# A graph layer on one core: a slot's rows loaded and split chunks ahead, and two small products placed behind slot products in TensorE's order

## The chip, the core and the metric

The kernel runs on one core of one Trainium2 chip. A core has five engines that run beside each other and wait for one another by semaphores: TensorE (PE) multiplies matrices, VectorE (DVE) and ScalarE (ACT) work element by element, GpSimd (POOL) here mostly issues indirect DMAs that gather rows, and SyncE (SP) issues plain DMAs. Each engine runs its own instructions strictly in the order in which they stand in its queue; an instruction that waits holds up all behind it. The metric is the device time of one execution in microseconds (us), the median of several runs.

## The reference

```python
def _L0_gnn_ref(x, src, dst, theta_w, theta_b, phi_w, phi_b):
    x_src = x[src]
    x_dst = x[dst]
    theta_x = (x_dst - x_src) @ theta_w.T + theta_b
    phi_x = x_src @ phi_w.T + phi_b
    e = jax.nn.relu(theta_x + phi_x)
    out = jax.ops.segment_max(e, dst, num_segments=x.shape[0])
    return jnp.where(jnp.isfinite(out), out, 0.0)
x = _layernorm(x + _L0_gnn_ref(x, src, dst, ...), axis=-1)
```

There are 6250 nodes of 256 float32 features and 100000 edges, sorted by destination. Every node takes the maximum, over its incoming edges, of a linear function of both ends, adds it to itself, and is normalised.

## The kernel before

**The algebra.** What an edge adds that depends on its source is one row, B[source] = x[source] @ (phi - theta).T. The part that depends on the destination is the same for all edges of a node and is added after the maximum. So the kernel makes B once (the DRAM tensor `b_rows`), and then needs, per node, the maximum of B over its sources.

**Three ways to the maximum.** The first 618 nodes ("part 1") gather one row per edge: `gather_group` issues indirect DMAs on POOL, eight steps to a group, and `run_steps` (L696) runs a capped maximum along the steps on DVE, 81 steps in all. The other 5632 nodes are served by **slots** and by the **list**. A slot is a block of 383 rows of B; there are 17. For each slot and each of these nodes at most one edge is chosen, and its row is fetched by a product with a one-hot matrix; the maximum is kept in `acc`. Edges that no slot took go to the list, which is gathered like part 1, 257 steps.

**A slot.** `slot_terms(s)` (L1063) loads the slot's rows from `b_rows` into `raw` (SP, L1078; one buffer), splits them into a rounded part (ACT, L1082) and the rest (DVE, L1083), and keeps both in `terms` (two buffers). `slot_halves(s, c)` then works on one **chunk** of the nodes: chunks 0 to 4 have 1024 nodes and chunk 5 has 512. It loads the chosen row numbers (`want`, three buffers), makes the one-hot tile `hot` (two buffers; ACT L1102 and L1105, or DVE L1100 for one block out of three once `dve_hots` is set), and for each half h of the features multiplies `terms` by `hot` into a PSUM tile `ps_f` (three buffers; 12 matmuls for a half of a wide chunk, 6 for a half of chunk 5; L1113), which DVE merges into `acc` (L1124; ACT L1122 in slot 0). I write "slot 2, chunk 0, half 1" for such a piece; slots count from 0. Of each block's two terms the rounded part is multiplied first, so the first two matmuls of a half need only ACT's part, and the third needs DVE's.

**The list's front.** While slots 0 to 3 run, DVE also finishes part 1's steps and builds the list (`list_pieces`): a sum over lists (`sums_of_lists`, two small matmuls at L1151 and L1152, whose result `list_chunks` reads), a compaction of a table of 1584 entries (L1244, L1254), a DMA of the compacted words (L1263), three indirect DMAs that fetch each partition's run of words (`dst_w`, L519), and DVE's merge of these (L1275 to L1286), whose result `list_src` releases the list's 256 gathers on POOL.

**The end of part 1.** `tails_1` takes the last row of each partition through TensorE (L905), a scan on DVE (L907) and a cap (L910), back through TensorE (L914) and into `carried` (ACT, L916), which `heads_1` uses at L925, after the list has begun.

**What sets the order.** The calls are written in one program order, but the framework that builds the program arranges each engine's queue itself, by its own estimate of when each operand is there. `behind_in_order(one, name, reason)` adds an order without a wait: `one` stands behind `name` on its engine. In the list's phase (`pinned`) the list's steps and the slots' merges on DVE are tied to each other in that way, and `halves_until` spreads the slots' pieces over the list's steps. At the end POOL gathers the 44 tiles' results from `maxima_2` and DVE and ACT normalise them.

## Time and profile before

| | before |
|---|---|
| runs | 739.37, 734.26, 736.09 us, median 736.09 |
| profiled execution | 738.83 us, of which the span of the core's instructions 737.0 us |
| PE / DVE / ACT / POOL busy | 90% / 86% / 72% / 72% of the span |
| mean granted clock of TensorE | 0.955 |
| slot matmuls (L1113) | 2156, 519.9 us busy |
| DMA | 167.06 MB, 227 GB/s over the span |

The page of the profile gives busy shares, the costliest groups of instructions with the idle time ahead of them, and the chain of work that ended last. A timeline row has start and length in us, the engine, the line of the kernel, the operation with its output and input tiles, the number of instructions merged into it, and in brackets the idle time ahead of it and what ended it. Since instructions overlap in an engine's pipeline, a row's length can be more than the distance to the next row's start. A row of a table by stretches has the stretch, its length, the busy time of PE, of its weight loads, of DVE, ACT and POOL with instruction counts, then the granted clock, the share of DMA and its GB/s.

### The profile page before, as it was taken

How to read it: one execution, taken by the hardware profiler on the slowest of the kernel's cores; microseconds unless marked ns; L12 is line 12 of the kernel's file. 1: busy time of each engine (PE TensorE's matmuls, PEld its weight loads, DVE VectorE, ACT ScalarE, POOL GpSimd, SP SyncE). 2: the span in 40 equal slices, each digit the busy share in tenths (PEclk: the TensorE clock that was granted, in tenths of full speed). 3: DMA queues.
4: the chain of work that ended last, by engine and by line, in shares of the span. 5: the costliest groups of instructions: out<-in, count | busy, mean ns of one | idle time of the engine just before them, and what ended most of it. 6: DMA issues, size and time to landing. Idle time of an engine off the chain costs nothing.

```text
span 737.0 us, 9895 instructions
## 1 busy us (share of the span) xinstructions
PE 661.5 (90%) x2908; PEld 536.1 (73%) x2908; DVE 630.5 (86%) x1193; ACT 532.7 (72%) x611; POOL 529.1 (72%) x730
## 2 busy tenths in 40 slices
PE   5989978679697999999999999999999988979990
PEld 3878756567475888888888888888888876758880
DVE  7999998999996678988989888888888984697885
ACT  1445788788697676967869687876877878852685
POOL 6810477888315848888888888888888888438880
PEclk9999998889798999999999999999999998989995
DMA  8997553737456547777787968786867675555874
GB/s 260 313 360 289 191 165 108 261 101 229 156 194 207 179 143 223 247 217 260 222 277 217 354 218 272 249 312 223 263 211 252 210 243 177 164 187 172 269 279 192
DMA packets 60879, 167.06 MB, mean 227 GB/s; under 512 B 11896, under 2 KB 21905, under 8 KB 54673
## 3 DMA queue, kind: packets, MB, share of 16 engines
q1 hardware_dynamic: 39717, 107.15, 41.6%
q0 software_dynamic: 18976, 52.35, 24.1%
q10 hardware_dynamic: 2124, 6.84, 2.5%
q8 instruction: 25, 0.41, 0.2%
q14 instruction: 37, 0.30, 0.1%
HBM read 102.94 MB, written 63.36 MB: 226 GB/s over the span
## 4 chain that ended last, share of the span: by engine, by line
PE 63%; DVE 11%; DMA 7%; ACT 7%; POOL 6%; issue 6%; SPq 0%; DVEq 0%; POOLq 0%; ACTq 0%
PE ps_f L1113 56%; PE ps_b L791 4%; POOL g L526 4%; DMA x_columns<-x_t 3%; DVE g L696 2%; ACT hot L1102 2%; ACT hot L1105 2%; DMA g<-maxima,place 2%; POOL pause L496 1%; DVE wide L1032 1%; DMA dst_w<-list_words,run_start 1%; DVE words L1244 1%; DVE acc L1124 1%; DMA w_in<-in_L_gnn_theta_w_dram 1%; ACT x_t L779 1%
## 5 line engine op out<-in xcount | busy, mean ns | idle before, releaser
L1113 PE MATMUL ps_f<-hot,terms 128*128 128x512 f32 x2156 | 519.9, 402 | 28.0 <-ACT hot L1105 22.0
L1113 PEld LDWEIGHTS ps_f<-hot,terms 128*128 128x128 f32 x2156 | 412.7, 194 | 128.8 <-ACT hot L1105 31.6
L526 POOL DMA_INDIRECT g<-b_rows,list_src x256 | 258.2, 1009 | 61.0 <-issue 37.3
L1102 ACT ACTIVATE hot<-want,minus_row 128x1024 fp32r<-128x1024 f16 (+1 forms) x224 | 229.0, 1071 | 97.7 <-PE ps_f L1113 97.7
L1124 DVE TENSOR_TENSOR acc<-acc,ps_f 128x1024 f32<-128x1024 f32 x192 | 215.8, 1129 | 69.4 <-PE ps_f L1113 68.6
L1105 ACT ACTIVATE hot<-hot 128x2048 fp32r<-128x2048 f32 (+2 forms) x102 | 196.4, 1925 | 2.5
L696 DVE SCALAR_TENSOR_TENSOR g<-g,caps 128x256 f32<-128x256 f32 x335 | 161.1, 481 | 2.1
L526 POOL DMA_INDIRECT g<-b_rows,src x65 | 89.4, 1376 | 62.8 <-DMA b_rows<-b_sb 43.0
L496 POOL IOTA pause<- 128x160 f32 x312 | 96.9, 311 | 2.3
L791 PE MATMUL ps_b<-weights,x_t 128*128 128x256 f32 x260 | 60.9, 388 | 2.8 <-ACT x_t L779 2.4
L526 POOL DMA_INDIRECT g<-maxima,place x44 | 42.7, 971 | 27.1 <-DMA maxima<-g 20.2
L791 PEld LDWEIGHTS ps_b<-weights,x_t 128*128 128x128 f32 x260 | 48.9, 194 | 11.3 <-ACT x_t L779 5.2
L1100 DVE TENSOR_SCALAR hot<-want,row_id 128x1024 fp32r<-128x1024 f16 (+1 forms) x70 | 52.1, 745 | 0.3 <-issue 0.3
L1363 PE MATMUL ps_e<-weights,kept 128*128 128x256 f32 x176 | 41.6, 379 | 0.0
L1393 ACT ACTIVATE squares<-x_f,r 128x256 bf16<-128x256 f32 x49 | 24.2, 494 | 20.6 <-DVE r L1390 20.6
L1363 PEld LDWEIGHTS ps_e<-weights,kept 128*128 128x128 f32 x176 | 33.4, 190 | 4.3
L794 ACT COPY b_sb<-ps_b 128x512 f32<-128x512 f32 (+1 forms) x25 | 14.4, 578 | 23.4 <-PE ps_b L791 16.8
L779 ACT COPY x_t<-ps_xt 128x512 f32<-128x512 f32 (+1 forms) x33 | 18.5, 588 | 13.1 <-PE ps_xt L776 7.8
L526 POOL DMA_INDIRECT g<-in_x_dram,src x16 | 23.1, 1444 | 5.4 <-issue 4.1
L1408 ACT ACTIVATE x_f<-x_f,r 128x256 f32<-128x256 f32 x41 | 21.4, 588 | 6.8 <-DVE r L1400 3.9
L1373 DVE TENSOR_TENSOR g<-g,ps_e 128x512 f32<-128x512 f32 x22 | 15.1, 686 | 8.7 <-DMA g<-maxima,place 3.5
L519 POOL DMA_INDIRECT dst_w<-list_words,run_start x3 | 3.1, 1048 | 25.8 <-DMA list_words<-work 25.5
(255 smaller groups left out, 429.6 us busy)
## 6 DMA issues: line engine op xcount, KB each, us to landing
maxima<-g SPq DMA_DIRECT2D x42, 1024.0 KB
want<-chosen_rows SPq DMA_DIRECT2D x85, 256.0 KB
x_q<-in_x_dram SPq DMA_DIRECT2D x12, 512.0 KB
b_rows<-b_sb ACTq DMA_DIRECT2D x12, 512.0 KB
x_columns<-x_t SPq DMA_DIRECT2D x22, 256.0 KB
kept<-x_columns SPq DMA_DIRECT2D x11, 512.0 KB
raw<-b_rows SPq DMA_DIRECT2D x16, 256.0 KB
g<-b_rows,list_src POOLq DMA_INDIRECT x256, 4.3
```

Source lines behind the costliest of these rows:

```text
L496: return nc.gpsimd.iota(t, pattern=[[step, t.shape[1]]], base=base, channel_multiplier=per_partition, allow_small_or_imprecise_dtypes=True,)
L526: one = nc.gpsimd.indirect_dma_start(out=to, out_offset=None, in_=table, in_offset=bass.IndirectOffsetOnAxis(ap=offsets, axis=0))
L696: one = nc.vector.scalar_tensor_tensor(g[:, k, :], last[part], caps[:, t : t + 1], g[:, k, :], op0=ALU.min, op1=ALU.max)
L779: nc.scalar.copy(x_t[:, :w], ps[:, :w])
L791: nc.tensor.matmul(ps[:, h, :], x_t[:, h, k, :], weights[:, k, 0, :], start=(k == 0), stop=(k == KC - 1))
L1100: nc.vector.tensor_scalar(hot[:, b, :], want, row_id[:, b : b + 1], None, op0=ALU.is_equal)
L1102: nc.scalar.activation(hot[:, b, :], want, AF.Abs, bias=minus_row[:, b : b + 1], scale=1.0)
L1105: nc.scalar.activation(apart, apart.bitcast(FP), AF.Relu, bias=1.0, scale=-1.0)
L1113: nc.tensor.matmul(ps[:, w : w + 512], terms[:, part, b, h * P : (h + 1) * P], hot[:, b, w : w + 512], start=(i == 0), stop=(i == n - 1),)
L1124: one = nc.vector.tensor_tensor(to, to, ps, op=ALU.max)
L1363: nc.tensor.matmul(a[:, i, :], x_t[:, 2 * i + c, :], weights[:, c, 1, :], start=False, stop=(i == w - 1 and c == KC - 1))
L1393: nc.scalar.activation(squares, x_f[:, k, :], AF.Square, bias=mean[:, k : k + 1], scale=1.0, accum_out=var[:, k : k + 1])
```

## The change

Two things are altered. First, `slot_terms` becomes a generator of two steps, rows and terms: the rows of slot s+1 are asked for at chunk 2 of slot s, its terms at chunk 4 of slot s; before, both were asked for at chunk 0 of the slot itself. Slot 0 still does both at once. Second, two small products on TensorE are issued later in the program and tied behind the latest slot product that has been written: the sums over the lists, and the transposes of the carried rows, which move from `tails_1` to the first step of `heads_1`, inside the list's loop. No instruction is added or removed.

```diff
+ROWS_AT = 2
+TERMS_AT = 4
...
+    latest_product = [None]
...
         nc.vector.memset(capped[:, :, 0:1], -BIG2)
+        return capped
+
+    def heads_1(capped):
         carry = misc()
         for k in range(KC):
-            nc.tensor.transpose(carry[:, k * P : (k + 1) * P], capped[:, k, :], ident)
+            one = nc.tensor.transpose(carry[:, k * P : (k + 1) * P], capped[:, k, :], ident)
+            behind_in_order(one, latest_product[0], "slots ahead of the heads")
         carried = work.tile([P, D], FP, name="carried", bufs=1)
         nc.scalar.copy(carried, carry[:, :D])
-        return carried
-
-    def heads_1(carried):
         heads = work.tile([P, D], FP, name="heads", bufs=1)
...
             if s == 0:
                 behind_in_order(one, x_loaded, "x ahead of a slot's rows")
+        yield
         terms = terms_of[s] = slots.tile([P, PARTS, KB, D], FR, name="terms")
         nc.scalar.copy(terms[:, 0, :n], raw[:, :n])
...
+        yield
+
+    terms_ahead = [None]
 
     def slot_halves(s, c):
-        if c == 0:
-            slot_terms(s)
+        if c == 0 and s == 0:
+            for _ in slot_terms(s):
+                pass
+        if c == ROWS_AT and s + 1 < NS:
+            terms_ahead[0] = slot_terms(s + 1)
+            next(terms_ahead[0])
+        if c == TERMS_AT and s + 1 < NS:
+            next(terms_ahead[0])
         terms, blocks = terms_of[s], blocks_in(s)
...
-                    nc.tensor.matmul(
+                    one = nc.tensor.matmul(
...
+            latest_product[0] = one.ins.name
             to = acc[:, h, begin : begin + wide_of]
...
+        return counts, tri
+
+    def sums_product(counts, tri):
+
         ps = misc()
-        nc.tensor.matmul(ps[:, :P], counts, tri, start=True, stop=True)
+        one = nc.tensor.matmul(ps[:, :P], counts, tri, start=True, stop=True)
+        behind_in_order(one, latest_product[0], "slots ahead of the sums")
         nc.tensor.matmul(ps[:, P : P + 1], tri, n_list, start=True, stop=True)
         return ps
...
-        list_chunks(sums)
+        list_chunks(sums_product(*sums))
...
-    carried = tails_1()
+    capped = tails_1()
...
-    heads = heads_1(carried)
+    heads = heads_1(capped)
```

What this does to the queues follows from the framework's arrangement. POOL's queue is the same row for row. From slot 6 on, the loads of rows stand where they stood on SP, but for one slot in the middle of the list's phase. Otherwise the queues differ in the stretch from slot 0 to slot 5. (In the changed kernel the lines are numbered 3 to 20 higher: L1083 is L1088, L1124 is L1139, L1113 is L1127, L905 is L908, L914 is L920, L1151 is L1170, L1261 is L1281.)

DVE's queue at the end of slot 1. The rows named `words` and `work` are the list's compaction, `g` are part 1's steps, `acc` with 1024 columns are chunk 4's merges of slot 1 and those with 512 columns are chunk 5's, and `terms` is slot 2's second part. Before:

```order
L1254 COPY_PREDICATED work_774<-words,work_774 128x1520 [waits DVE_49]
L696 TENSOR_SCALAR g<-g,caps_171 128x256 [waits DMASW0_49,DVE_49]
L1124 TENSOR_TENSOR acc<-acc,ps_f 128x512 [waits PE_49,Activation_49]
L696 TENSOR_SCALAR g<-g,caps_171 128x256 [waits DMASW1_49,DVE_49]
L1124 TENSOR_TENSOR acc<-acc,ps_f 128x512 [waits PE_49,Activation_49]
L696 TENSOR_SCALAR g<-g,caps_171 128x256 [waits DMAHW3_49,DMASW2_49,DVE_49]
L1244 TENSOR_SCALAR words<-work_774 128x1456
L696 TENSOR_SCALAR g<-g,caps_171 128x256 [waits DMASW3_49,DVE_49]
L1254 COPY_PREDICATED work_774<-words,work_774 128x1456 [waits DVE_49]
L696 TENSOR_SCALAR g<-g,caps_171 128x256 [waits DMASW4_49,DVE_49]
L1083 TENSOR_TENSOR terms<-raw,terms 128x768 [waits DMAHW2_49,DMAHW0_49,Activation_49]
```

And with the change:

```order
L1264 TENSOR_SCALAR words<-work_774 128x1552
L699 TENSOR_SCALAR g<-g,caps_171 128x256 [waits DMASW5_49,DVE_49]
L1274 COPY_PREDICATED work_774<-words,work_774 128x1552 [waits DVE_49]
L699 TENSOR_SCALAR g<-g,caps_171 128x256 [waits DMASW6_49,DVE_49]
L1088 TENSOR_TENSOR terms<-raw,terms 128x768 [waits DMAHW2_49,DMAHW3_49,DMAHW0_49,Activation_49]
L699 TENSOR_SCALAR g<-g,caps_171 128x256 [waits DMASW7_49,DVE_49]
L1139 TENSOR_TENSOR acc<-acc,ps_f 128x1024 [waits PE_49]
L699 TENSOR_SCALAR g<-g,caps_171 128x256 [waits DMASW0_49,DVE_49]
```

Slot 2's second part has moved from behind slot 1's last merge, and behind two more rounds of the compaction, to a place ahead of chunk 4's merges of slot 1.

PE's queue where slot 1 ends and slot 2 begins; the number behind `ps_f` is the PSUM tile, one for each half of a chunk, and `terms_1652` (before) and `terms_1572` (changed) belong to slot 2. Before:

```order
L1113 MATMUL ps_f_1631<-hot_1626,terms_1372 128x512 x6
L1113 MATMUL ps_f_1639<-hot_1626,terms_1372 128x512 x6
L1113 MATMUL ps_f_1662<-hot_1657,terms_1652 128x512 x2
L1113 MATMUL ps_f_1676<-hot_1657,terms_1652 128x512 x2
L1113 MATMUL ps_f_1717<-hot_1712,terms_1652 128x512 x2
L1113 MATMUL ps_f_1662<-hot_1657,terms_1652 128x512 x10
L1113 MATMUL ps_f_1676<-hot_1657,terms_1652 128x512 x10
L1113 MATMUL ps_f_1717<-hot_1712,terms_1652 128x512 x10
```

With the change:

```order
L1127 MATMUL ps_f_1637<-hot_1632,terms_1282 128x512 x6
L1127 MATMUL ps_f_1645<-hot_1632,terms_1282 128x512 x6
L1127 MATMUL ps_f_1662<-hot_1657,terms_1572 128x512 x12
L1127 MATMUL ps_f_1676<-hot_1657,terms_1572 128x512 x12
L1127 MATMUL ps_f_1717<-hot_1712,terms_1572 128x512 x12
```

Before, three halves of slot 2 (both of chunk 0 and one of chunk 1) began with the two matmuls that need only ACT's part, and were finished afterwards; now each half is done in one piece.

PE's queue where slot 2 ends and slot 3 begins. Before, the last rows of part 1 (`g`) and the carried rows (`capped`) stood together ahead of slot 3's first half:

```order
L1113 MATMUL ps_f_1887<-hot_1874,terms_1652 128x512 x6
L905 MATMUL ps_2090<-ident_84,g_1786 128x128 x2
L914 MATMUL ps_2098<-ident_84,capped_2095 128x128 x2
L1113 MATMUL ps_f_1908<-hot_1903,terms_1898 128x512 x12
L1113 MATMUL ps_f_1922<-hot_1903,terms_1898 128x512 x12
```

With the change:

```order
L1127 MATMUL ps_f_1893<-hot_1880,terms_1572 128x512 x6
L908 MATMUL ps_2093<-ident_84,g_1789 128x128 x2
L1127 MATMUL ps_f_1908<-hot_1903,terms_1840 128x512 x12
L1127 MATMUL ps_f_1922<-hot_1903,terms_1840 128x512 x12
L1127 MATMUL ps_f_1950<-hot_1945,terms_1840 128x512 x12
L1127 MATMUL ps_f_1964<-hot_1945,terms_1840 128x512 x12
L1127 MATMUL ps_f_1988<-hot_1983,terms_1840 128x512 x12
L1127 MATMUL ps_f_2002<-hot_1983,terms_1840 128x512 x12
L1127 MATMUL ps_f_2033<-hot_2028,terms_1840 128x512 x12
L1127 MATMUL ps_f_2047<-hot_2028,terms_1840 128x512 x12
L920 MATMUL ps_2135<-ident_84,capped_2098 128x128 x2
```

The transposes of the carried rows have moved behind eight halves of slot 3. The sums over the lists have moved less: they stood ahead of a node's place product (L858) in slot 0, between chunks 3 and 4, and now stand behind it at the same spot.

## The prediction

> **What bounds the kernel now.** I read the table by stretches of 50 us first, then the chain that ended last, then TensorE's timeline where it idles, and last the rows of ACT, DVE and POOL beside it.

> ```profile
> 150.00:200.00 50.00, 41.11 (x150) 30.68 (x151) 48.40 (x60) 40.21 (x39) 34.68 (x24) 0.85 0.53 171
> 200.00:250.00 50.00, 43.39 (x177) 34.32 (x176) 38.05 (x97) 38.30 (x31) 23.32 (x35) 0.93 0.59 194
> 250.00:300.00 50.00, 50.00 (x220) 40.61 (x220) 39.09 (x57) 37.52 (x31) 34.26 (x53) 1.00 0.54 169
> ```

> TensorE is full from 250 us on; ahead of that it loses 8.89 us in one stretch and 6.61 in the next, at a clock of 0.85 and 0.93. From 150 to 200 us it is DVE that is full (48.40 of 50). The chain, in order of time, goes over to TensorE and stays there:

> ```profile
> 235.12 131.40 PE ps_f L1113 x564
> ...
> 655.50 0.95 POOL g L526
> ```

> From 235 us the slot products run back to back, the list's steps are tied to them on DVE, and the last gathers (POOL, from 655.50) follow the list's end. So what TensorE gains ahead of 235 us moves everything behind it by as much. The question is where slot 3's first product, at 234.77, comes to stand.

> ```profile
> 132.04 0.80 PE L1151 MATMUL ps<-src_w 128*128 128x128 f32 x2 [3.83 <-DVE src_w L1149]
> ...
> 150.41 7.96 PE L1113 MATMUL ps_f<-hot,terms 128*128 128x512 f32 x24 [3.09 <-ACT hot L1105]
> ...
> 184.66 1.66 PE L1113 MATMUL ps_f<-hot,terms 128*128 128x512 f32 x6 [0.53 <-DVE acc L1124]
> 188.90 0.91 PE L1113 MATMUL ps_f<-hot,terms 128*128 128x512 f32 x2 [2.58 <-ACT hot L1105]
> 190.60 1.22 PE L1113 MATMUL ps_f<-hot,terms 128*128 128x512 f32 x2 [0.79 <-DVE acc L1124]
> 194.81 12.74 PE L1113 MATMUL ps_f<-hot,terms 128*128 128x512 f32 x44 [3.00 <-ACT hot L1105]
> 208.70 5.73 PE L1113 MATMUL ps_f<-hot,terms 128*128 128x512 f32 x24 [1.14 <-ACT hot L1105]
> 214.62 5.73 PE L1113 MATMUL ps_f<-hot,terms 128*128 128x512 f32 x24 [0.19 <-ACT hot L1105]
> 220.57 8.58 PE L1113 MATMUL ps_f<-hot,terms 128*128 128x512 f32 x36 [0.21 <-ACT hot L1105]
> 228.98 0.38 PE L905 MATMUL ps<-ident,g 128*128 128x128 f32 x2
> 234.43 0.69 PE L914 MATMUL ps<-ident,capped 128*128 128x128 f32 x2 [5.06 <-DVE capped L910]
> 234.77 15.44 PE L1113 MATMUL ps_f<-hot,terms 128*128 128x512 f32 x55
> ```

> 184.66 is slot 1's last half. At 188.90 and 190.60 slot 2's first two halves do two matmuls each and stop; then chunks 0 and 1 are finished in one piece from 194.81. Chunks 2 and 3 start at 208.70 and 214.62, chunks 4 and 5 at 220.57. The 24 matmuls of a wide chunk take 5.73 us, and 7.96 after an idle stretch, at 150.41.

> ```profile
> 182.81 3.23 ACT L1102 ACTIVATE hot<-want,minus_row 128x1024 fp32r<-128x1024 f16 x3 [2.46 <-PE ps_f L1113]
> 186.08 2.76 ACT L1105 ACTIVATE hot<-hot 128x3072 fp32r<-128x3072 f32 x1
> ...
> 200.96 0.83 ACT L1082 CAST terms<-raw 128x768 fp32r<-128x768 f32 x1 [6.20 <-DMA raw<-b_rows]
> 202.61 3.23 ACT L1102 ACTIVATE hot<-want,minus_row 128x1024 fp32r<-128x1024 f16 x3 [0.82 <-PE ps_f L1113]
> 205.88 2.77 ACT L1105 ACTIVATE hot<-hot 128x3072 fp32r<-128x3072 f32 x1
> ...
> 226.35 4.27 ACT L1102 ACTIVATE hot<-want,minus_row 128x1024 fp32r<-128x1024 f16 x4 [2.48 <-PE ps_f L1113]
> 230.53 2.75 ACT L1105 ACTIVATE hot<-hot 128x3072 fp32r<-128x3072 f32 x1
> ```

> ACT needs 6.04 us for a one-hot tile (182.81 to 188.84), and with two tiles it cannot begin one before TensorE is through with the chunk two earlier. So in this stretch the pace is ACT's, and a late chunk 0 makes a late tile for chunk 2: it was begun at 202.61, ready at 208.65.

> **The change, part by part.** *Slot 2's terms.*

> ```profile
> 183.39 1.21 DVE L1124 TENSOR_TENSOR acc<-acc,ps_f 128x1024 f32<-128x1024 f32 x1
> 184.52 0.48 DVE L696 SCALAR_TENSOR_TENSOR g<-g,caps 128x256 f32<-128x256 f32 x1
> 184.92 1.22 DVE L1124 TENSOR_TENSOR acc<-acc,ps_f 128x1024 f32<-128x1024 f32 x1
> ...
> 195.11 0.97 DVE L1083 TENSOR_TENSOR terms<-raw,terms 128x768 fp32r<-128x768 f32 x1
> 195.98 0.50 DVE L696 SCALAR_TENSOR_TENSOR g<-g,caps 128x256 f32<-128x256 f32 x1
> ...
> 213.28 0.48 DVE L1261 TENSOR_TENSOR work<-work,owner 128x316 int32<-128x316 int32 x1
> ```

> Slot 2's second part was made at 195.11, 6.3 us after its chunk 0 could start (188.84). In the new queue it stands ahead of slot 1's chunk-4 merge, the one at 183.39. By start-to-start distances a merge costs DVE 1.13, a step 0.40, the terms 0.87. Ahead of that merge now also stand the terms, some three more steps and two short rows of a node's place (each under a step's 0.40): about 2.5 us, so the merge begins near 185.9 and is done at 187.0. Slot 1's last half needs that merge's PSUM tile: it starts at 187.1, not 184.66, and ends at 188.5. That costs nothing, because chunk 0's one-hot tile is ready only at 188.84.

> From there slot 2 runs whole halves. TensorE has by then idled most of the 4.2 us since 184.7, so I price chunk 0 with the row of 150.41, 8.0 us: 188.9 to 196.9. ACT begins chunk 2's tile then: 3.23 + 2.77 + the cast of slot 3's rounded part (0.7 between starts) gives 203.6 against 208.65: **5.1 us gained**. ACT's wait of 6.20 us for `raw` goes too: the load waited for the terms at 196.11 and now follows them near 186. Chunks 2 to 5 keep their distance to slot 3's tile (208.65 to 233.28), since DVE's merges of slot 2 come 0 to 3 us ahead of the halves that need their tiles.

> *The carried rows.* Slot 3's tile was ready at 233.28 (230.53 + 2.75), but the product waited behind L914 until 234.77: **1.5 us gained**. What is late next is that tile, not the last step of part 1, which I put at 226 on DVE. The two transposes now stand in the full stretch and cost there what L905's two cost, 0.4 us.

> *The sums.* They keep their place between chunks 3 and 4 of slot 0, only behind the place product that had followed them. Their wait of 3.83 us for DVE's L1149 ends when it did; then two products stand ahead of chunk 4 instead of one, between nothing and 0.8 us (132.04). Half of that is lost again in the wait for ACT's tile: 0.3 us lost.

> *The list's front.* L1261 (213.28) now stands behind three more merges and 2.5 us of other rows, less waits that go: I put it at 217.

> ```profile
> 228.35 0.95 POOL L526 DMA_INDIRECT g<-b_rows,list_src  x1 [6.78 <-DVE dst_w L1281]
> ...
> 266.86 1.22 POOL L526 DMA_INDIRECT g<-b_rows,list_src  x1 [9.76 <-DVE g L696]
> ```

> The list's gathers began 15.07 us after L1261, so they begin near 232, 3.7 us later. That is hidden: the gathers waited 9.76 us at 266.86 for a list step to free their rows.

> *The rest.* After 250 us the order is the same but for one slot's terms in the full stretch, at no cost while TensorE is full.

> The sum: -5.1 - 1.5 + 0.4 + 0.3 = **-5.9 us**. Against the profiled 738.83 that is 732.9. The median of the runs, 736.09, lies 2.74 lower, so I forecast **730.2 us**.

> **The clock.** TensorE's clock is 0.85 in the stretch with the many short idles. The row of 150.41 (7.96 us after 3.09 us of idle) and that of 214.62 (5.73 after 0.19) bound chunk 0 of slot 2 between 8.0 and 5.7 us; the bounds from both places where TensorE restarts are 2.2 us better and about 1 us worse than the sum. [...]

> **The rivals.**
> (a) *The clock holds* at slot 2's start: chunk 0 takes 5.73, 2.2 us more are gained, 728.0. For it: the idle is broken by six matmuls. Against it: 190.60's two matmuls after 2.58 us of idle took 1.22 us, at 188.90 two took 0.91.
> (b) *The change moves what it says, and DVE takes it back.* DVE is full until 200 us; if its merges are 2 to 3 us later than I have them, slot 2's halves wait for PSUM tiles instead of for terms, and only the carried rows' 1.5 us less 0.7 remain: 735.3. For it: DVE's 48.40 of 50. Against it: the wait for `acc` in TensorE's rows is 0.53 and 0.79.
> (c) *Slower, through the list's front.* DVE now waits for the fetched runs ahead of slot 4's terms and of slot 3's first merge, and PSUM has three tiles: chunk 1's second half of slot 3 stalls until that merge. I expect the last run at 229.3 and need the merge, 3.2 us behind that, by 238.8 (slot 3's start at 228.1, plus 8.0 for a cold chunk and half of 5.7): 6.3 us of slack, then 1 us per us. If the 15.07 us chain took twice as long, 8.8 us would be lost and 5.9 gained: 739.0. Against it: the same DMAs with the same traffic took 15.07.

> **How the numbers follow.** Forecast 0.55, (a) 0.18, (b) 0.19, (c) 0.08. The forecast's own range is 728 to 732.5 (one term each way). The range over the cases reaches from 725.8 (the clock holds at both restarts: 736.1 - 5.9 - 2.2 - 2.2) to 737 ((b) with nothing left, and the first part of (c)). About 1%, 7.4 us, is what a measurement of this kernel tells from no change: 728.7 and 743.5. Faster by more than 1% are (a), most of it, and the forecast's lower end: 0.33. Slower by more are only long delays under (c): 0.05. Within 1%: 0.63.

> **What would show it.** Slot 2's chunks as whole groups of 24 from about 189; its terms on DVE near 185; ACT's cast of slot 3's part with no wait for `raw`; chunk 2 of slot 2 at 203 to 204; slot 3's first product at 228 to 229 with no wait for `capped`; the list's first gather at 231 to 233, and no 9.76 us wait behind it; the list's end and the last gathers 5 to 7 us earlier. I am wrong if TensorE waits for `acc` in slot 2 for more than 1 us at a time, if DVE waits for rows of `g` in the list's phase, or if the tail behind the list's end changes length.

## The result and the profile after

The changed kernel takes **729.04 us** (median of 4 runs, 727.97 to 729.96) beside 736.0 us for the kernel before: a ratio of 0.988 with a 95% interval from 0.985 to 0.991. A second comparison further down gives 0.988 again (0.985 to 0.991; 729.82 beside 738.65 us). So 7.0 and 8.8 us are gained; the forecast was 5.9, and 730.2 us. The profiled execution took 729.61 us, its span is 727.8 us.

Three stretches of 50 us, with the columns of the prediction's first rows:

```profile
150.00:200.00 50.00, 42.66 (x173) 33.32 (x174) 47.69 (x63) 45.30 (x43) 41.75 (x26) 0.94 0.54 173
200.00:250.00 50.00, 45.58 (x190) 35.84 (x189) 44.52 (x104) 40.80 (x31) 20.52 (x31) 0.97 0.61 198
250.00:300.00 50.00, 50.00 (x221) 40.56 (x220) 41.66 (x65) 38.83 (x34) 42.85 (x65) 1.00 0.65 205
```

TensorE is still full from 250 us on. Ahead of that it idles 7.34 and 4.42 us instead of 8.89 and 6.61, and its clock is 0.94 and 0.97 instead of 0.85 and 0.93. The chain of waits, in order of time, goes over to TensorE 7.3 us earlier than before (235.12 there):

```profile
202.97 5.99 PE ps_f L1127 x24
208.98 3.25 ACT hot L1116 x3
212.25 2.78 ACT hot L1119
215.08 7.96 PE ps_f L1127 x34
225.02 2.76 ACT hot L1119
227.83 23.65 PE ps_f L1127 x96
251.69 107.10 PE ps_f L1127 x468
```

Ahead of 227.83 the chain alternates between ScalarE's one-hot tiles (`hot`) and the products that use them. TensorE's timeline around slots 1 to 3:

```profile
134.08 0.72 PE L861 MATMUL ps<-ids,hot 128*128 128x83 f32 x2 [5.07 <-DVE hot L859]
...
151.82 0.79 PE L1127 MATMUL ps_f<-hot,terms 128*128 128x512 f32 x1 [6.16 <-ACT hot L1119]
...
178.59 7.09 PE L1127 MATMUL ps_f<-hot,terms 128*128 128x512 f32 x30 [0.86 <-ACT hot L1119]
188.67 7.52 PE L1127 MATMUL ps_f<-hot,terms 128*128 128x512 f32 x30 [2.99 <-DVE acc L1139]
197.05 5.76 PE L1127 MATMUL ps_f<-hot,terms 128*128 128x512 f32 x24 [0.85 <-ACT hot L1119]
202.97 11.71 PE L1127 MATMUL ps_f<-hot,terms 128*128 128x512 f32 x48 [0.16 <-ACT hot L1119]
215.08 8.45 PE L1127 MATMUL ps_f<-hot,terms 128*128 128x512 f32 x36 [0.40 <-ACT hot L1119]
225.69 0.44 PE L908 MATMUL ps<-ident,g 128*128 128x128 f32 x2 [2.16 <-DVE g L699]
227.83 22.50 PE L1127 MATMUL ps_f<-hot,terms 128*128 128x512 f32 x91 [1.70 <-ACT hot L1119]
```

The 30 products from 188.67 are slot 1's last half (6) and slot 2's chunk 0 (24): no half stops in its middle any more, and 30 products in 7.52 us are 0.25 each, at a granted clock of 1.00 (187.13 to 200.79). Slot 3 begins at 227.83, and no `capped` is waited for. ScalarE's timeline beside it, with slot 2's one-hot tiles and the cast of slot 3's rounded part:

```profile
184.36 3.23 ACT L1116 ACTIVATE hot<-want,minus_row 128x1024 fp32r<-128x1024 f16 x3 [2.46 <-PE ps_f L1127]
187.62 2.78 ACT L1119 ACTIVATE hot<-hot 128x3072 fp32r<-128x3072 f32 x1
190.37 3.23 ACT L1116 ACTIVATE hot<-want,minus_row 128x1024 fp32r<-128x1024 f16 x3
193.50 0.82 ACT L1087 CAST terms<-raw 128x768 fp32r<-128x768 f32 x1
...
196.90 3.21 ACT L1116 ACTIVATE hot<-want,minus_row 128x1024 fp32r<-128x1024 f16 x3
200.14 2.77 ACT L1119 ACTIVATE hot<-hot 128x3072 fp32r<-128x3072 f32 x1
```

VectorE's timeline, with slot 2's terms, the merge behind them, the end of the list's compaction and, later, the first shares of the output:

```profile
186.14 0.95 DVE L1088 TENSOR_TENSOR terms<-raw,terms 128x768 fp32r<-128x768 f32 x1
...
187.41 1.21 DVE L1139 TENSOR_TENSOR acc<-acc,ps_f 128x1024 f32<-128x1024 f32 x1
...
217.90 0.48 DVE L1281 TENSOR_TENSOR work<-work,owner 128x316 int32<-128x316 int32 x1
...
374.91 0.42 DVE L1394 TENSOR_TENSOR x_f<-x_f,ps 128x256 f32<-128x256 f32 x1 [1.01 <-DMA x_f<-maxima,place]
...
414.00 0.69 DVE L1394 TENSOR_TENSOR x_f<-x_f,ps 128x512 f32<-128x512 f32 x1 [1.92 <-DMA x_f<-maxima,place]
```

GpSimd's timeline, with the list's first gather, the one wait for a list step that is left, and the first of the last gathers:

```profile
231.91 0.95 POOL L528 DMA_INDIRECT g<-b_rows,list_src  x1 [5.83 <-DVE dst_w L1301]
...
273.90 0.96 POOL L528 DMA_INDIRECT g<-b_rows,list_src  x1 [1.94 <-DVE g L699]
...
647.23 0.95 POOL L528 DMA_INDIRECT g<-maxima,place  x1 [18.16 <-DMA maxima<-g]
```

From 184.36 on ScalarE does one tile after another without a wait; its 6.20 us wait for `raw` is gone. Slot 2's second part stands at 186.14, ahead of the merge at 187.41. GpSimd's 9.76 us wait for a list step has shrunk to 1.94, and the last gathers begin 8.3 us earlier (655.50 before). VectorE's waits for rows of `x_f` have grown: the one at 374.91 is new, the one at 414.00 was 0.71 us before (at 420.55).

**How the profiles are compared.** Slot 1's first product stood anywhere from 148.93 to 153.78 us in the 14 profiles of this study, though nearly the same work stands ahead of it (only the sums' place differs, and e9 and e10 have 12 products more). So a difference of one or two us between two spans says nothing by itself; what I compare is the distance, within one profile, from slot 1's first product (S1) to slot 3's first (S3), and from there to the end of the list's steps on VectorE. Each number is the start of a timeline row; the list's end is the start of the last row of steps plus its length.

| kernel | ratio (95%) | S1 | S3 | S1 to S3 | list's end | S3 to list's end |
|---|---|---|---|---|---|---|
| before | 1 | 150.41 | 234.77 | **84.36** | 650.5 | 415.7 |
| changed | 0.988 (0.985-0.991) | 151.82 | 227.83 | **76.01** | 642.2 | 414.4 |
| changed, again (e12) | 0.988 (0.985-0.991) | 149.87 | 225.53 | **75.66** | 639.8 | 414.3 |
| terms alone (e1) | 0.989 (0.986-0.992) | 148.93 | 224.96 | **76.03** | 642.0 | 417.0 |
| transposes alone (e2) | 1.000 (0.998-1.002) | 150.08 | 233.14 | **83.06** | 647.6 | 414.5 |
| sums alone (e3) | 1.012 (1.009-1.014) | 153.39 | 244.91 | **91.52** | 660.0 | 415.1 |
| without the sums (e4) | 0.987 (0.984-0.990) | 151.76 | 227.62 | **75.86** | 643.1 | 415.5 |
| terms at chunk 5 (e5) | 0.990 (0.986-0.994) | 151.49 | 231.10 | **79.61** | 646.0 | 414.9 |
| the same, filled (e6) | 0.991 (0.989-0.994) | 151.32 | 230.91 | **79.59** | 645.2 | 414.3 |
| runs late (e7) | 0.996 (0.994-0.999) | 153.78 | 229.68 | **75.90** | 650.5 | 420.8 |
| blocks on VectorE (e8) | 0.985 (0.982-0.989) | 150.59 | 223.78 | **73.19** | 637.9 | 414.1 |
| gaps filled (e9) | 0.990 (0.987-0.993) | 151.16 | 226.74 | **75.58** | 643.3 | 416.6 |
| e8 and slot 1's gap (e10) | 0.988 (0.985-0.991) | 150.35 | 221.74 | **71.39** | 636.4 | 414.7 |
| sums alone, x behind (e11) | 1.001 (0.999-1.003) | 152.15 | 238.96 | **86.81** | 652.8 | 413.8 |

From the list's end to the end of the span it is 84.9 to 86.5 us in all of them (88.0 in e10). The changed kernel's gain is thus the 8.35 us between S1 and S3, plus 1.3 and 0.9 us behind it, less 1.4 us by which this execution reached slot 1 later: 9.2 us between the two spans.

### The profile page after: what moved, and what is told of

It reads as the page before. It is cut to its first block, busy times and chain, and to the rows that moved or that the text cites. A ratio compares the mean times of both kernels' runs of the same rounds, so it can differ in the third digit from the quotient of the medians.

```text
span 727.8 us, 9889 instructions
## 1 busy us (share of the span) xinstructions
PE 654.3 (90%) x2908; PEld 530.6 (73%) x2908; DVE 630.3 (87%) x1193; ACT 531.7 (73%) x611; POOL 531.2 (73%) x730
## 4 chain that ended last, share of the span: by engine, by line
PE 58%; DVE 17%; ACT 9%; POOL 6%; issue 5%; DMA 3%; DVEq 0%; SPq 0%; POOLq 0%; ACTq 0%
PE ps_f L1127 57%; POOL g L528 5%; ACT hot L1119 3%; ACT hot L1116 3%; DVE g L699 2%; DVE words L1003 2%; DVE wide L1036 2%; DVE work L1000 1%; POOL pause L498 1%; ACT x_f L1428 1%; DVE unused L1050 1%; DMA g<-maxima,place 1%; DVE wide L1046 1%; DMA dst_w<-in_dst_dram,window 1%; DVE wide L1032 1%
## 5 line engine op out<-in xcount | busy, mean ns | idle before, releaser
L1127 PE MATMUL ps_f<-hot,terms 128*128 128x512 f32 x2156 | 513.3, 398 | 28.4 <-ACT hot L1119 20.7
L1127 PEld LDWEIGHTS ps_f<-hot,terms 128*128 128x128 f32 x2156 | 407.8, 191 | 127.0 <-ACT hot L1119 30.5
L1139 DVE TENSOR_TENSOR acc<-acc,ps_f 128x1024 f32<-128x1024 f32 x192 | 215.7, 1129 | 58.1 <-PE ps_f L1127 57.1
L528 POOL DMA_INDIRECT g<-b_rows,src x65 | 95.1, 1463 | 70.0 <-DMA b_rows<-b_sb 50.1
L528 POOL DMA_INDIRECT g<-in_x_dram,src x16 | 18.5, 1157 | 5.5 <-issue 4.1
```

Of the source, the lines that this page charges most:

```text
L528: one = nc.gpsimd.indirect_dma_start(out=to, out_offset=None, in_=table, in_offset=bass.IndirectOffsetOnAxis(ap=offsets, axis=0))
L1127: one = nc.tensor.matmul(ps[:, w : w + 512], terms[:, part, b, h * P : (h + 1) * P], hot[:, b, w : w + 512], start=(i == 0), stop=(i == n ...
L1139: one = nc.vector.tensor_tensor(to, to, ps, op=ALU.max)
```

## The experiments

**Which part gains: terms alone (e1), transposes alone (e2), sums alone (e3), all but the sums (e4).** Each takes the changed kernel and puts the other parts back where they stood. e1 and e4 keep the early rows and terms, e2 and e3 put them back:

```diff
-        if c == 0 and s == 0:
+        if c == 0:
             for _ in slot_terms(s):
                 pass
-        if c == ROWS_AT and s + 1 < NS:
-            terms_ahead[0] = slot_terms(s + 1)
-            next(terms_ahead[0])
-        if c == TERMS_AT and s + 1 < NS:
-            next(terms_ahead[0])
```

e2 and e4 keep the transposes of the carried rows in `heads_1`, e1 and e3 put them back into `tails_1`; e3 alone keeps the late sums:

```diff
         carry = misc()
         for k in range(KC):
-            one = nc.tensor.transpose(carry[:, k * P : (k + 1) * P], capped[:, k, :], ident)
-            behind_in_order(one, latest_product[0], "slots ahead of the heads")
+            nc.tensor.transpose(carry[:, k * P : (k + 1) * P], capped[:, k, :], ident)
...
-        list_chunks(sums_product(*sums))
+        list_chunks(sums)
```

> Only the slots' rows and terms are made early; the sums over lists and the carried rows' transposes stand where they stood before. By the prediction's sum: 5.1 us gained, 736.0 - 5.1 = 730.9, slot 3's first product near 229.7. Rival, from the trace of the changed kernel: there part 1's last step on VectorE ends at about 225.6, and before the change the transposes of the carried rows came 5.06 us behind the transposes of the tails, so with the transposes left in place slot 3's first product is held up to 231 to 232: only some 3 us gained, 733, with a wait of 3 to 5 us for capped ahead of the transposes.

> Only the transposes of the carried rows are put behind slot 3's products; terms and sums as before the change. By the prediction: 1.5 gained at slot 3's first product, 0.4 paid for the transposes in the full stretch: 734.9. Rival: the tile of slot 3 is not what comes next, and the gain is nothing (736) or the clock's step at 233.8 moves with the idle and gives 2 to 3 us (733).

> Only the sums over lists are issued later, behind the slot's latest product; terms and transposes as before the change. By the prediction: 0.3 lost, 736.3. Rival, from the trace of the changed kernel: slot 0's last chunks began 1.6 us later there than before, of which 0.7 to 0.8 already stood at 118 us, so the later sums cost 0.8 us and show as 736.8; by the third reading they cost the whole 1.6 us, 737.6.

> Terms and transposes as in the changed kernel, the sums where they stood before the change. By the prediction: 736.0 - 5.1 - 1.5 + 0.4 = 729.8, that is 0.3 better than its own sum. Rival (the sums cost 0.8 to 1.6 us of the measured gain of 7.0): 727.4 to 728.2, better than the changed kernel. If slot 2's pace is ScalarE's alone, its first one-hot tile comes that much earlier, near 189 and not 190.4.

Measured: e1 729.9 us, e2 737.07, e3 746.61, e4 728.63, beside 737.82 for the kernel before. **The terms alone bring all of the gain** (0.989, as the whole change), the transposes alone none that can be measured, and the sums alone lose 8.5 us (by the ratio; the medians are 8.8 apart). Neither theory for e1 came true: it gains 7.9 us, where 5.1 and 3 were expected, and it has no wait for `capped` ahead of slot 3. TensorE in e1:

```profile
184.16 1.67 PE L1126 MATMUL ps_f<-hot,terms 128*128 128x512 f32 x6 [1.64 <-DVE acc L1138]
187.27 5.91 PE L1126 MATMUL ps_f<-hot,terms 128*128 128x512 f32 x24 [1.44 <-ACT hot L1118]
...
222.78 0.44 PE L908 MATMUL ps<-ident,g 128*128 128x128 f32 x2 [2.12 <-DVE g L699]
224.96 23.66 PE L1126 MATMUL ps_f<-hot,terms 128*128 128x512 f32 x96 [1.74 <-ACT hot L1118]
248.46 0.38 PE L917 MATMUL ps<-ident,capped 128*128 128x128 f32 x2
```

The transposes of the carried rows (L917) stand behind 96 of slot 3's products, though their code is that of the kernel before. The framework arranges TensorE's queue by its own estimates, and with slot 2's terms early it puts the transposes there by itself. In e2, where the edit does it, the distance from S1 to S3 shrinks by 1.30 us, near the 1.5 of the prediction, but the ratio's interval (0.998 to 1.002) is wider than that.

In e3 the queue is arranged otherwise at one more place:

```profile
236.01 0.38 PE L917 MATMUL ps<-ident,capped 128*128 128x128 f32 x2
244.60 0.66 PE L1368 MATMUL ps<-ident,x_f 128*128 128x128 f32 x2 [8.21 <-DMA x_f<-in_x_dram]
```

L1368 are the first transposes of x's own rows. In the kernels before and after 564 slot products stand between slot 3's first one and these; here they stand ahead of it, and TensorE waits 8.21 us for a DMA that nothing had hurried.

**Is it that place (e11), and does the result hold (e12)?** e11 is e3 with one order more:

```diff
                         one = nc.tensor.transpose(ps[:, 2 * i + c, :], x_f[:, k + i, c * P : (c + 1) * P], ident)
+                        if first_x[0]:
+                            behind_in_order(one, latest_product[0], "slots ahead of x")
+                first_x[0] = False
```

> The kernel with the sums' move alone, and the first transposes of x's rows (which stood ahead of slot 3's products in that kernel's order and waited 8.21 us for their DMA) are put behind TensorE's latest slot product. If that place is what made the sums' move alone slower by 8.5 us: slot 3's first product no longer waits for them but for its one-hot tile, 4.8 us earlier, and the ratio falls from 1.0115 to about 1.005; if it is all of the loss, 1.0004 by the prediction's 0.3 us; if the sums' move itself costs the 8.5 us, 1.0115 stays.

> The changed kernel once more, on the chip and beside the runs of the kernel before that the three other kernels share. All theories: a ratio of 0.988, and slot 3's first product 76.0 us behind slot 1's. A ratio above 0.992 or a distance other than 76.0 by over 0.3 us would say that the first profile was not a typical one.

Measured: e11 739.88 us, e12 729.82, beside 738.65. With these transposes behind the products most of the loss of the sums' move is gone: the ratio is 1.001 (0.999 to 1.003), and S3 stands 4.7 us nearer to S1 than in e3, as expected. So most of e3's 8.5 us are an effect of the arrangement and not a cost of the two products. Not all of it is explained. From S1 to S3 e11 still takes 2.45 us more than the kernel before: slot 2's terms stand 45.9 us behind S1 in e11 and in e3, where it was 44.7 before, and slot 2's chunk 2 starts 60.4 and 60.3 us behind S1, where it was 58.3. No run shows why, and a loss of up to 2 us fits into the interval.

What the sums cost in front of slot 1 is measured at S1: from the start of the last transpose ahead of them (L892 before the change, L895 behind it) it is 25.67, 25.34, 26.08, 25.69 and 25.68 us to S1 where the sums stand as before (before, e1, e2, e4, e8), and 26.46, 26.12, 26.38, 25.87, 26.90, 26.08 and 26.12 where they are moved (changed, e3, e11, e12, e5, e6, e7): 0.6 us more on average, with ranges that overlap. e12 confirms the changed kernel's time. Its distance, 75.66, lies 0.34 us from the 76.0 expected, a little more than the 0.3 named there; beside the differences read here, of 1.3 us and more, that is small.

**The place of the terms (e5), and idle time filled (e6).**

```diff
-TERMS_AT = 4
+TERMS_AT = 5
```

e6 has this too, and ahead of slot 2's first half products that nobody reads:

```diff
+        if s == 2 and c == 0:
+            filler = misc()
+            for i in range(8):
+                nc.tensor.matmul(filler, terms_of[1][:, 0, 0, :P], hot_before[0][:, 0, :512], start=True, stop=True)
```

> The changed kernel with one number changed: a slot's terms are made at chunk 5 of the slot before, not at chunk 4, so VectorE reaches both chunk-4 merges of slot 1 ahead of slot 2's terms; TensorE's order is unchanged. If the split of the idle time by slot 1's last half is what held TensorE's clock at slot 2's start, the last half now follows at once, the idle time of some 3 us stands in one piece, the clock drops, slot 2's chunk 0 takes near 8.0 us instead of 5.9, and slot 3's first product comes 1.4 us later (ScalarE is free 1.4 us before chunk 0 would end): 77.4 us behind slot 1's first product instead of 76.0, 730.4. If the idle time has nothing to do with it (the place of the terms decides): chunk 0 takes 5.9 and 76.0 stays, 729. If terms one chunk later are too late for slot 2: chunk 0 stops in its middle as it did before the change, and 2 us or more are lost.

> As the run with terms at chunk 5, and TensorE multiplies eight times more (operands of slot 1, the product is read by nobody) ahead of slot 1's last half: 1.9 us of the idle time are filled and no other engine has more to do. By the clock theory the clock holds, chunk 0 of slot 2 takes 5.9 us and slot 3's first product stands 76.0 us behind slot 1's, against 77.4 in the run without the filling. By the rival (the clock does not matter, the place of the terms does) both runs give the same distance.

Measured: 732.07 and 732.44 us beside 739.62. What came true is the third case of e5, terms that are too late, in e5's timeline of TensorE:

```profile
190.31 0.73 PE L1127 MATMUL ps_f<-hot,terms 128*128 128x512 f32 x2 [1.41 <-ACT hot L1119]
193.44 12.33 PE L1127 MATMUL ps_f<-hot,terms 128*128 128x512 f32 x46 [2.40 <-DVE terms L1088]
```

Behind chunk 4's merges VectorE came to the terms only at 192.43, and chunk 0 stopped after two products for 2.40 us. One chunk later costs 3.6 us of the 8.35 (79.61 instead of 76.01). e6 gave the same distance: the filling stood ahead of the stop and not in it, and the clock dropped at 193.2 us in e6 as at 194.1 in e5. So the pair says nothing on the clock; e9 does.

**The slack of the list's front (e7).** In the kernel that ran there were 24 pauses, not the 40 that the expectation names; they took 8.50 us.

```diff
         for i, to in enumerate((list_edges, second, third)):
+            if i == 2:
+                for _ in range(24):
+                    in_turn(nc.gpsimd.iota(pause, pattern=[[0, PAUSE]], base=0, channel_multiplier=0, allow_small_or_imprecise_dtypes=True))
             gather_run(to, list_words, run_start[:, i : i + 1])
```

> The changed kernel with 40 more pauses (0.45 us each, 18 us in all) on GpSimd ahead of the third fetched run of the list: list gathers begin near 250 and not 232, and VectorE's order has slot 3's first merges ahead of the wait for that run. By the prediction's account of the list's front, a late start of the gathers is hidden: here by what is left, 1.94 us of waiting on GpSimd and the least distance of 11.15 us between a gather's issue and its step, less about 4.3 us for landing, 8.8 us in all; so about 9 us are lost, 738. If the list's front has no slack, 18 us are lost, 747; if the gathers catch up, none, 729.

The first list gather came at 240.18, 86.40 us behind S1, which is 6.3 later than in the changed kernel (231.91 - 151.82 = 80.09). By the rule in the text, with 8.8 us hidden, nothing should be lost. Measured: 736.54 us beside 739.62, a ratio of 0.996 where the changed kernel has 0.988, and 6.4 us more from S3 to the list's end (420.8). So about as much as the delay is lost, and not where I had looked. The list's steps had their rows in time (the least distance from a gather's issue to its step is 7.9 us). VectorE's waits for `x_f` in e7:

```profile
380.92 0.42 DVE L1397 TENSOR_TENSOR x_f<-x_f,ps 128x256 f32<-128x256 f32 x1 [4.88 <-DMA x_f<-maxima,place]
...
422.56 0.69 DVE L1397 TENSOR_TENSOR x_f<-x_f,ps 128x512 f32<-128x512 f32 x1 [4.45 <-DMA x_f<-maxima,place]
```

And TensorE's first wait behind them, for what VectorE makes of these rows (`r`):

```profile
383.02 2.98 PE L1127 MATMUL ps_f<-hot,terms 128*128 128x512 f32 x12 [1.78 <-DVE r L1413]
```

Between the list's gathers GpSimd issues a few that fetch finished maxima for the first shares of the output (`x_f`), and VectorE waits for them in its own order, ahead of merges that TensorE needs. In e7 TensorE stops for VectorE three times there, for 1.78, 1.61 and 1.78 us (at 383.02, 387.62 and 424.98). In the changed kernel the same two waits for `x_f` are 1.01 and 1.92 us and stop TensorE nowhere between 230 and 590 us; in the kernel before only the second was there:

```profile
420.55 0.69 DVE L1374 TENSOR_TENSOR x_f<-x_f,ps 128x512 f32<-128x512 f32 x1 [0.71 <-DMA x_f<-maxima,place]
```

The other profiles show how little slack the changed kernel has left. Its list gathers begin 4.1 us behind S3, e12's 4.5, and TensorE does not stop. In e1 and e4 they begin 4.9 and 5.0 us behind S3; there the first wait for `x_f` is 3.10 and 2.95 us, and TensorE stops once for 1.7 us, so that the long block of products behind these waits starts 212.6 and 212.4 us behind S3 and not 210.5 as in the changed kernel. In e7, e8 and e10 it is 10.4 to 11.2 us, with waits of 4.8 to 5.0. So less than 1 us seems to be left, though no run moved the gathers by so little.

**A version that goes further (e8), the clock (e9), and both (e10).** e8 is e4 with VectorE making one of three blocks of `hot` from slot 3's first chunk and until the end. e9 is e4 with 12 products in TensorE's idle time ahead of slot 1 and 8 ahead of slot 3; e10 is e8 with the 12.

```diff
             held[0] = True
-            fetch_parts(AHEAD_OF_RUNS)
+            fetch_parts(AHEAD_OF_RUNS - 1)
+            dve_hots[0] = DVE_HOTS
+            fetch_parts(1)
...
-            dve_hots[0] = 0
```

e9 and e10 fill as e6 does, but behind the latest product and ahead of the slots named:

```diff
+                behind_in_order(one, latest_product[0], "products ahead of the filling")
```

> The version without the sums' move, and VectorE makes one of the three blocks of the one-hot tile from slot 3's first chunk on (not from its second) and until the end (not until the last groups of the list). If what is late at slot 3's start is ScalarE's one-hot tile and nothing else, that tile takes 4.1 us and not 6.9, slot 3's first product comes about 2 us earlier, and the 4.17 us wait ahead of the last slot's products becomes about 2: 728.6 - 4 = 724.6. Rival: VectorE, which makes the blocks, is the bound there and merges come later, no gain or a loss: 728.6 to 731.

> The version without the sums' move, and TensorE multiplies 12 times ahead of slot 1's first product and 8 times ahead of slot 3's (operands of the slot before; the products are read by nobody), 2.9 and 1.9 us of its idle time at full clock; nothing else changes. If a drop of TensorE's clock behind an idle stretch is worth what the prediction took it for: without the filling slot 1's first 24 products took 8.00 us and slot 3's first stretch ran at half clock for 3 to 3.5 us; with it slot 1's chunk takes 5.73 and ScalarE's tile for chunk 2 starts 1.9 us earlier (its wait there), so slot 3's first product stands 74.0 us behind slot 1's instead of 75.86, and 1.5 us more are gained behind it: 3.4 us, a ratio of 0.982. If ScalarE and VectorE set the pace at both places and TensorE's clock is beside the point: 75.86 stays, 0.987. If the filling itself is late and pushes the products: up to 1 us lost, 0.988.

> The version in which VectorE makes one of three blocks from slot 3's first chunk until the end, and the 12 products that fill TensorE's idle time ahead of slot 1. If slot 1's clock is worth 1.9 us: 0.9852 less 0.0026, 0.983, with slot 3's first product 71.3 us behind slot 1's instead of 73.2. If VectorE's merges hold TensorE there, 73.2 and 0.985.

Measured: e8 728.62 us beside 739.62; e9 731.45 and e10 729.52 beside 738.65. In e8 the tile was what was late at slot 3's start: S3 comes 2.7 us earlier than in e4 (73.19 instead of 75.86). The 4.17 us wait ahead of the last slot is gone, but TensorE now waits 5.07 us for one of VectorE's merges ahead of its last 20 products. Where 4 us were expected, the intervals of e8's 0.985 and e4's 0.987 show no difference. In e8 and e10 the first waits of VectorE for `x_f` are 5.04 and 4.76 us, as in e7, and there the gain at S3 is handed back: from S3 to the long block of products behind these waits it is 217.3 us in e8, where it was 212.4 in e4. In e10 the distance from S1 to S3 is the expected one (71.39 for 71.3), the ratio is not (0.988 for 0.983). None of these beats the changed kernel by more than the runs can tell.

e9 shows the clock. Its timeline of TensorE (L1125 is the filling):

```profile
148.31 3.01 PE L1125 MATMUL ps<-hot,terms 128*128 128x512 f32 x12
151.16 5.61 PE L1135 MATMUL ps_f<-hot,terms 128*128 128x512 f32 x24
...
185.86 1.76 PE L1135 MATMUL ps_f<-hot,terms 128*128 128x512 f32 x6 [2.26 <-DVE acc L1147]
188.36 13.86 PE L1135 MATMUL ps_f<-hot,terms 128*128 128x512 f32 x48 [0.74 <-ACT hot L1121]
202.93 5.78 PE L1135 MATMUL ps_f<-hot,terms 128*128 128x512 f32 x24 [0.70 <-ACT hot L1121]
```

And in e4, without the filling:

```profile
151.76 8.00 PE L1127 MATMUL ps_f<-hot,terms 128*128 128x512 f32 x24 [3.13 <-ACT hot L1119]
...
190.28 5.98 PE L1127 MATMUL ps_f<-hot,terms 128*128 128x512 f32 x24 [1.42 <-ACT hot L1119]
...
203.00 5.73 PE L1127 MATMUL ps_f<-hot,terms 128*128 128x512 f32 x24 [0.20 <-ACT hot L1119]
```

Slot 1's chunk 0 now takes 5.61 us and not 8.00, as expected. Slot 2's chunk 0 starts 1.32 us nearer to S1 for it (37.20 us behind it, 38.52 in e4). But the granted clock then dropped to one half at 187.26, at slot 2's start, where in e4 it had held, and more than this gain was lost there: from chunk 0's first product to chunk 2's it is 14.57 us in e9 (188.36 to 202.93) and 12.72 in e4 (190.28 to 203.00). From there to S3 0.81 us come back, so that 0.28 us are left at S3, where 1.9 were expected. Of the 1.5 us expected behind S3 nothing came: it is 416.5 us to the list's end and 415.5 in e4. So 1.85 us is the price of a dropped clock at slot 2's start in this pair. The prediction's cold figure for this stretch, 203.6 - 188.84 = 14.76, is what e9 shows, and the changed kernel, where chunk 0's tile was ready at 190.40 and chunk 2's first product stands at 202.97, has 12.57.

## Why the prediction was right, and where it was not

**Right: what bounds, and where the gain is.** It is TensorE's early start on slot 3, and behind S3 the time moves little (413.8 to 417.0 us to the list's end, e7 apart). Slot 2's terms stand at 34.3 us behind S1 (186.14 - 151.82; forecast 34.6, by "near 185"), slot 1's last half begins 36.85 behind S1 (forecast 36.7, by 187.1), and chunk 0's tile is ready 38.6 behind S1, as before (38.4). The new wait for `acc` (2.99 us at 188.67) costs nothing, as said, since the tile came at 190.40. ScalarE's wait for `raw` is gone, and the tail kept its length to 0.9 us. Three of the signs named lie just outside what was said, all on the side of a larger gain: chunk 2 of slot 2 at 202.97 (203 to 204), S3 at 227.83 (228 to 229), the last gathers 8.3 us earlier (5 to 7).

**The step that failed: "I price chunk 0 with the row of 150.41, 8.0 us".** Chunk 0 of slot 2 ran at a granted clock of 1.00 in the changed kernel and in e1, e4, e7, e8 and e12 (24 products in 5.91 us in e1, 5.98 in e4). So ScalarE, without a pause from 184.36 on, set the pace, and chunk 2's tile was ready 51.1 us behind S1 (202.91) and not 53.2 (203.6 - 150.41): **7.15 us gained, not 5.1**. This is rival (a), "the clock holds", to which I gave 0.18, and its 728.0 us lies 1.0 below the median. That 730.2 lies only 1.2 above it is in part luck: between S1 and S3 the sum was short by 2.15 us, and of the 8.8 us of the second comparison the forecast has two thirds. I had called (a) less likely because two matmuls after 2.58 us of idle took 1.22 us at 190.60. The 2.58 us stand ahead of the row of 188.90, and ahead of 190.60 it is 0.79; the clock was at one half from 189.29. In the kernel before, the row of 190.60 stood behind a window in which TensorE had been busy for 0.83 of 3.41 us; here slot 1's last half, held back by the merge, falls into the middle of the gap, a window there (187.13 to 190.55) was busy for 1.75 of 3.42 us, and the clock held. That the one made the other is not shown (below).

**The carried rows: the size was right, the cause was not.** From chunk 2's tile to S3 it is 26.12 us before (208.65 to 234.77) and 24.92 after (202.91 to 227.83): 1.2 gained where I had 1.5 less 0.4. But I put it down to the edit of the transposes, and e1 has it without that edit (24.71, from 200.25). An estimate-driven arrangement had made the second edit unnecessary.

**The sums.** 0.3 us lost were forecast, 0.6 on average were measured ahead of S1, and leaving the move out gains nothing that can be told (e4 beside the change). That the same move alone would turn TensorE's queue at another place and lose most of 8.5 us there no term of the sum could have said: I had costed each edit by its own instructions.

**The sum** from S1 to S3 is then -7.15 - 1.2 = -8.35 us for -5.1 - 1.5 + 0.4 = -6.2. The medians show 7.0 and 8.8 us. That the start of slot 1, later by 0.6 us for the sums, and the runs' own scatter make the difference is how I read it; it is not shown. Two small slips in the working change nothing: 228.1 + 8.0 and half of 5.7 is 238.95 and not 238.8, and the three shares by 1% add up to 1.01.

**The list's front.** Gathers from 231.91 on (forecast 231 to 233), L1281 at 217.90 (217), the 9.76 us wait gone: right. "That is hidden" is right for the changed kernel, but hardly anything is left behind it: 6.3 us more cost 6.4 (e7), and e1 and e4 already pay 2 us there. Rival (c) saw the danger at slot 3's first merge; it lies some 140 us later, at the rows of `x_f`. Rival (b), VectorE taking the gain back, did not occur in the changed kernel: no half of slot 2 waits for a PSUM tile. What VectorE coming to the terms one chunk later would have cost is measured by e5: 3.6 us.

## What to carry to other kernels

Move an operand's preparation ahead of the operations that free the consumer, and look at how many us it stands ahead of its use: here chunk 4 of the slot before is in time by some 3 us and chunk 5 late by 2.4. Where a framework arranges the queues by estimates, compare the arranged queues of each edit and not only the edit: one of three did by itself what another was written for, and the third alone cost 8.5 us, most of it at a place that it does not touch. And when a stage is made earlier, ask which in-order queue now runs behind it, GpSimd's here, since the next us gained is lost there.

## What the runs showed of the hardware that I had not expected

```profile
187.13:190.55 3.42, 1.75 (x7) 1.15 (x7) 3.42 (x6) 3.39 (x3) 2.67 (x3) 1.00 0.76 235
```

The same window in e12, the changed kernel once more:

```profile
184.59:188.01 3.42, 1.58 (x6) 1.05 (x6) 3.42 (x6) 3.39 (x2) 2.69 (x3) 1.00 0.65 202
```

And in e9, with the gaps filled:

```profile
183.85:187.26 3.41, 1.40 (x6) 1.05 (x6) 3.41 (x6) 3.38 (x3) 2.52 (x3) 1.00 0.80 252
```

With 1.75 and 1.58 us busy (51% and 46%) the clock held, with 1.40 (41%) it dropped. In e4, at the place of e9's window (183.86 to 187.27), it was 1.71 us (50%), and the clock held. Over all 14 profiles (100 to 258 and 594 to 660 us) the shortest busy time in a window at full clock with no drop behind it is e12's 1.58 us, and the longest with a drop behind it is 1.75 us, in the changed kernel (118.87 to 122.28). At half clock the shortest with a rise behind it is 2.83 us (e9, 112.17 to 115.58), the longest with none 2.97 us (e2, 131.26 to 134.67). So some 3 us of idle time at the same place cost nothing in e4 and 1.85 us in e9, where the windows began 32.10 and 32.69 us behind S1; that may be a part of the scatter between executions. What decides whether the clock drops is not shown: no run set the busy share of a window alone.
